# Router logits computed from split token blocks instead of plain tokens, in a fused linear-attention and router kernel

## The chip, the core and the metric

The kernel runs on one core of a Trainium2 chip. A core has five engines that run side by side, each taking its own instructions strictly in order, tied to the others only by semaphores: TensorE (PE in the profile; its weight loads are a row of their own, PEld), VectorE (DVE), ScalarE (ACT), GpSimd (POOL) and SyncE (SP), which here only issues transfers. Matrix products land in eight PSUM banks of 128 x 512 float32. The metric is the device time of one execution in microseconds (us); the profile adds one execution taken apart.

## The reference

Input x is four sequences of 512 tokens with 512 features. After a layer norm, xn goes two ways. One is a decayed linear attention with 16 heads of width 128 (queries, keys, values are silu of projections; a sigmoid gate; an output projection). The other is a router, whose logits the change touches:

```python
logits = jnp.einsum('th,eh->te', flat, router_weight) + router_bias   # 64 experts
scores = jax.nn.softmax(logits, axis=-1)
topk_w, topk_idx = jax.lax.top_k(scores, TOP_K)                       # 8 of 64
out = flat * jnp.sum(topk_w, axis=-1, keepdims=True) + jnp.einsum('tk,tkh->th', topk_w, expert_bias[topk_idx])
```

The result is x + attention * silu(router output).

## The kernel before, in words

**Split products.** Every big product is done in TensorE's float32r form, on numbers split in two: ScalarE casts the high part (`split_hi`, L99, rows of L100), VectorE or GpSimd subtracts it for the low part (`split_lo`, rows of L103). A product takes three passes: high with high, low with high, high with low (`PASSES`, L27).

**Seven products for eight.** The sequences are worked on in two pairs, p = 0 and 1 (`PB` = 2). With the features halved and the two sequences of a pair as the other half, each projection is a 2 x 2 product of blocks: B11 and B12 are the two sequences' first halves of features, B21 and B22 their second halves. It is done in the seven products of `PRODUCTS` (L39) with sums of weights (S1 to S4) and of tokens: T1 = B12 - B11, T2, T3, T4. `unit` (L484) runs the seven, product 0 to product 6, six matmuls each, into three PSUM banks. Product 4 adds onto the bank of product 1, product 5 onto that of product 2, product 6 onto that of 1 and 4. So product 4 waits until VectorE has read its addition "a" from that bank, product 5 until it has read "e", product 6 until it has read the sum of product 4. "a" also needs s1, ScalarE's copy of product 0 (L508).

**Hooks.** A unit takes `after`, seven lists; list i is emitted behind product i. All side work is put there by hand, and that decides its place in each engine's queue. `do_deferred` (L563) emits silu products (VectorE) that wait for ScalarE's sigmoid.

**The v stage** (loop at L947, to about 187 us of the span) has 16 units k = 0 to 15 of 128 tokens from each sequence of a pair. Units 0 to 7 use the first half of the value weights, with p = 0, then p = 1; units 8 to 15 the second half, with p = 1, then p = 0. The first two units are plain products (`plain_unit`, L525; rows of L534) while the weight sums S1 to S4 are being made (`sum_of`, L421; `split_one`, L444; L970 to L975). Units 0 to 6 also prepare the tokens ahead: transposes of tile k + 1 ("turn", rows of L251), ScalarE's copies into xf, sums T1 to T4 on GpSimd (ts, L268), statistics and normalisation of tile k + 2 on VectorE (bn, L226; x, L202; GpSimd makes rstd, L236, in between), splits of the blocks (ACT L100, POOL L103), and the logits. The blocks of p = 1 stay in place at the end of unit 7; from unit 9 those of p = 0 are made again, tile by tile (`combine`), and are complete after unit 12. The value outputs go through four buffers with the tag "vout" to memory.

**Logits before** (`logits`, L310; rows of L318 and L323): for each tile and each sequence, four plain float32 matmuls with the tokens (xf, 128 features x 128 tokens) as the stationary operand and the router weights (128 x 64) as the moving one, so that tokens land on partitions. VectorE adds the bias. Later come the maximum and its subtraction (`scores_less`, L328), the exponentials, and the stores to memory (`scores_exp`, L337), in unit 13. Each exponential on ScalarE needs a table load, and so does going back to sigmoids.

**After the v stage** come units for gate, queries and keys with the attention of the head before (`attention`, L727), each with `scores_qk` (L670), `states` and `attend`; then the output projection (`o_head`, L824; rows of L826), between whose first heads the last head's attention is done (`last_steps`, L1108). `scores_qk` puts scores ("sa") and transposed keys ("kt") into a ring of three banks (`ps_sc`); `attend` has a bank of its own (`ps_o`).

The only lines needed word for word:

```python
lambda: scores_qk(b1, h, attp), lambda: scores_qk(b0, h, attp, (ps_o, "o")),   # L731, heads 0 to 14
[lambda: scores_qk(b1, hl, attp), lambda: scores_qk(b0, hl, attp)],               # L1109, last head
```

Of the kernel before, what the change touches and what calls it, by code (L numbers as in the profile page):

```python
# [18 lines left out]
PB = 2  # L19
# [31 lines left out]
def kernel(  # L51
# [41 lines left out]
    ps_sc = pool(ctx, "ps_sc", 3, space=PSUM)  # L93
    ps_o = pool(ctx, "ps_o", 1, space=PSUM)
# [4 lines left out]
    def split_hi(hi, src):  # L99
        nc.scalar.copy(hi, src)  # L100

    def split_lo(eng, lo, src, hi):
        eng.tensor_tensor(lo, src, hi.bitcast(F32), ALU.subtract)  # L103
# [40 lines left out]

    def warm_up(n):
        ps = ps_o.tile([P, P], F32, tag="o", name="warm")
        for _ in range(n):
            nc.tensor.transpose(ps, ident, ident)  # L150


    def make_dist():
# [36 lines left out]
    blocks = {}  # L190
# [51 lines left out]
    xfs = {}  # L242
# [62 lines left out]
            nc.sync.dma_start(out=blocks_d[n][:, t], in_=blocks[p, n].bitcast(F32)[:, t])  # L305


    lg = {}

    def logits(stage, p, t, js=range(PB)):  # L310
        if t == 0 and 0 in js:
            scores[p] = stage.tile([P, PB, NT, E], F32, tag="scores", name=f"scores_{p}", bufs=2)
        if 0 in js:
            lg[p, t] = ps_sc.tile([P, PB, E], F32, tag="sc", name=f"lg_{p}_{t}")
        ps = lg[p, t]
        for j in js:
            for c in range(FC):
                nc.tensor.matmul(  # L318
                    ps[:, j], xfs[p, t][:, j, c, :], rw[:, c, :], start=(c == 0), stop=(c == FC - 1)
                )  # L320
        if PB - 1 not in js:
            return
        nc.vector.tensor_tensor(  # L323
            scores[p][:, :, t, :], ps, rb[:, None, :].to_broadcast([P, PB, E]), ALU.add
        )


    def scores_less(p, what):  # L328
        sc = scores[p].rearrange("p b t e -> p (b t) e")
        if what == "top":  # L330
            scores[p, "top"] = small.tile([P, PB * NT], F32, tag="top", name=f"top_{p}", bufs=2)
            nc.vector.reduce_max(scores[p, "top"], sc, axis=AX.X)
        else:
            top = scores[p, "top"][:, :, None].to_broadcast([P, PB * NT, E])
            nc.vector.tensor_tensor(sc, sc, top, ALU.subtract)
# [334 lines left out]
    def scores_qk(b, h, attp, psum=(ps_sc, "sc")):  # L670
        s, d = (b, h), dec[b // PB, h]
        q, k = chunks(qs[s]), chunks(ks[s])
        pa = ps_sc.tile([P, NT, P], F32, tag="sc", name=f"sa_{b}_{h}")
        for c in range(NT):
            nc.tensor.matmul(pa[:, c], k[:, c], q[:, c], start=True, stop=True)  # L675
        pk = psum[0].tile([P, NT - 1, P], F32, tag=psum[1], name=f"kt_{b}_{h}")
        for c in range(NT - 1):
            nc.tensor.transpose(pk[:, c], k[:, c], ident)  # L678
        at[s] = attp.tile([P, NT, P], F32, tag="at", name=f"at_{b}_{h}")
        nc.vector.tensor_tensor(  # L680
            at[s], pa, d[:, 0, None, :].to_broadcast([P, NT, P]), ALU.mult
        )
# [154 lines left out]
    def prepare(stage, p, t):  # L837
        first = (p, t) == (0, 0)

        def turn():  # L840
            for j in range(PB):
                transpose(stage, p, j, t)
            if p == 0:
                nc.sync.dma_start(out=xf_d[t], in_=xfs[p, t])

        if p == 0 and t < NP_FIRST:
            sums = (lambda: plain(p, t, nc.vector if t == 0 else nc.gpsimd)), lambda: None, lambda: None
        else:
            sums = combine(stage, p, t, nc.gpsimd)

        def route_logits():
            logits(stage, p, t)
        return {
            "stats": lambda: layer_norms(p, t, first), "norms": lambda: normalise_x(p, t),
            "turn": turn, "sums": sums[0], "plain": sums[1], "more": sums[2], "logits": route_logits,
        }

    def h_units(p, stack):
# [78 lines left out]
    split_blocks(0, 0, nc.vector, (("T1", b12), ("B21", b21), ("B22", b22)))  # L937
    ws[0].split_one("A12", nc.vector, 0)
    ws[0].split_one("A12", nc.gpsimd, 1)
    logits(stage, 0, 0, [0])  # L940
    prep[1]["stats"]()
    prep[1]["norms"]()
    ws[0].split_one("A21", nc.vector)
# [2 lines left out]

    for k, (p, t) in enumerate(tiles + again):  # L947
        g, after = k // n1, nothing()
        for unit_of, what in ((n1 - 3, (0, "top")), (n1 - 2, (0, "less")), (n1 + 2, (1, "top")), (n1 + 3, (1, "less"))):
            if k == unit_of:  # L950
                after[2].append(lambda what=what: scores_less(*what))
        if n1 - NT <= k < n1:
            after[6].append(lambda p=p, t=t: keep_blocks(p, t))
        if k + 1 < n1:
            after[0 if k else 1].append(prep[k + 1]["turn"])
            if 0 < k < n1 - 3:
                after[0].append(lambda k=k: load_pair(stage, *tiles[k + 3]))
            if k == 0:
                after[1].insert(0, prep[2]["stats"])
            after[1].append(prep[k + 1]["sums"])  # L960
            if k + 2 < n1:
                if k:
                    after[1].append(prep[k + 2]["stats"])
                after[4 if k > 1 else 3].append(prep[k + 2]["norms"])
            after[1].append(prep[k + 1]["plain"])
            after[4].append(prep[k + 1]["more"])
            after[4 if k else 6].append(prep[k + 1]["logits"])
        if k == 0:
            after[0].append(lambda: logits(stage, 0, 0, [1]))
        if k < NP_FIRST:  # L970
            for i in range(2 * k, 2 * k + 2):
                after[2 + 2 * (i % 2)].append(lambda i=i: ws[0].sum_of(i, nc.vector))
            for i, n in enumerate((("S1", "S2"), ("S3", "S4"))[k]):
                eng = nc.gpsimd if i else nc.vector
                after[2 * i + 3].append(lambda n=n, eng=eng: ws[0].split_one(n, eng))  # L975
        if k == NP_FIRST:
            after[0].append(ws[1].load())
        if n1 - 5 <= k < n1 - 1:
            after[3].append(lambda n=k - n1 + 5: ws[1].sum_of(n, nc.vector))
        for n, unit_of, step, eng, piece in (  # L980
            ("A11", n1 - 2, 6, nc.gpsimd, None), ("S2", n1 - 1, 0, nc.gpsimd, None),
            ("S1", n1 - 1, 1, nc.gpsimd, None), ("A12", n1 - 1, 2, nc.vector, 0),
            ("S3", n1 - 1, 3, nc.gpsimd, None), ("A12", n1 - 1, 4, nc.vector, 1),
            ("S4", n1, 1, nc.vector, 0), ("S4", n1, 2, nc.vector, 1), ("A22", n1, 0, nc.gpsimd, None),
        ):
            if k == unit_of:
                after[step].append(lambda n=n, eng=eng, piece=piece: ws[1].split_one(n, eng, piece))
        if n1 <= k < n1 + NT:
            after[0].append(lambda t=t: load_xf(stage, t))
        if n1 < k <= n1 + NT:  # L990
            sums, split_plain, split_sums = combine(stage, 0, k - n1 - 1, nc.gpsimd, "r")
            after[1] += [sums, split_plain]
            after[4].append(split_sums)
        if k == NP_FIRST:
            after[0].append(keep_rows)
        if n1 + NT < k < n1 + 2 * NT:
            for j in range(1, len(PRODUCTS)):
                h = (k - n1 - NT - 1) * (len(PRODUCTS) - 1) + j - 1
                if h < NH:
                    after[j].append(lambda h=h: keep_decay(h))  # L1000
        if k == n1 + NT + 1:
            after[1].append(scores_exp)
        if k == 2 * n1 - 2:
            vs_stack.close()
            todo = [(p, *u) for p in range(NP) for u in h_units(p, hw_stack)]
            todo[0][3].load()()
            todo[1][3].load()()
        if k == 2 * n1 - 1:
            weight_steps(todo[0][3], after)
        v_unit(p, g, t, ws[g], vout, after, k < NP_FIRST)  # L1010
# [36 lines left out]
    for i, (p, kind, n, w) in enumerate(todo):  # L1047
# [58 lines left out]
    b1, b0 = B - 1, B - 2  # L1106
    hl = NH - 1
    last_steps = [  # L1108
        [lambda: scores_qk(b1, hl, attp), lambda: scores_qk(b0, hl, attp)],  # L1109
        [lambda: states(b1, hl, attp), lambda: states(b0, hl, attp)],  # L1110
        [lambda: attend(b1, hl, attp), lambda: attend(b0, hl, attp, (ps_sc, "sc"))],
    ]
# [98 lines left out]
```

## Time and profile before

| what | value |
|---|---|
| median of 3 runs | 1064.81 us (1064.03 to 1066.74) |
| profiled execution, its own time | 1063.93 us |
| its span (first to last instruction) | 1062.2 us |
| TensorE clock granted | 0.999 |
| chain that ended last | PE 87%, DVE 1%, all others about 0% |
| old logits, PE rows | 128 records from 9.1 to 97.8 us |
| transfers | 143.11 MB, mean 135 GB/s |

The v units start, by their first weight load, at 9.86 (k = 0), 24.94, 38.49, 51.48, 63.75, 76.00, 88.26, 100.53 (k = 7), 110.05, 120.29, 129.82, 139.34, 148.86, 158.38, 167.90 and 177.42. The next stage begins at 186.94.

How to read it: a row of the profile names the engine, the line of the kernel, the operation, the tile written, the tiles read, the shapes and a count. In a timeline the first two numbers are start and length in us; merged rows have a count, and their length runs from the first start to the last end. What stands in square brackets is the idle time of that engine just before, and what ended it. Rows of one engine may overlap slightly, since the next starts while the last drains: a VectorE row of 0.68 holds its queue for about 0.60. In a table of busy time by stretch the columns are the stretch, its length, and the busy time of PE, PEld, DVE, ACT and POOL, each with its number of instructions.

### The profile page before, as it was taken

To read this page: it belongs to the slowest core of one execution; us is meant where nothing else is said; L and a number is where in the kernel's file an instruction comes from. 1 tells how busy PE (TensorE), PEld (TensorE's weight loads), DVE (VectorE), ACT (ScalarE), POOL (GpSimd) and SP (SyncE) were. 2 spreads that over 40 slices of the span, in tenths; PEclk is the share of its full clock that TensorE was granted. 3 is DMA by queue.
4 is the path that set the end of the run, shared out by engine and by line. 5 is a ranking of instruction groups with operands and counts; after the bars stand their busy time and mean duration, and the time that the engine had idled before them with its cause. 6 is when DMAs were issued, how large, how long until landed. Compare 5 with 4: busy or idle time off the path is not lost.

```text
span 1062.2 us, 16490 instructions
## 1 busy us (share of the span) xinstructions
PE 1053.3 (99%) x5771; PEld 909.4 (86%) x5771; DVE 696.0 (66%) x1061; ACT 476.3 (45%) x923; POOL 728.7 (69%) x710
## 2 busy tenths in 40 slices
PE   9999999999999999999999999999999999999998
PEld 8888788888888888888888888888888888888886
DVE  7898876667576667665756656557566566855464
ACT  5555554544444444444444444444444444332221
POOL 5898893867787678777786787777867857612130
PEclk9999999999999999999999999999999999999999
DMA  6547747522422323235722242232222436455351
GB/s 225 188 176 251 261 148 234 163 85 86 139 85 95 98 92 109 85 124 180 271 85 72 83 125 85 85 123 82 94 72 83 154 128 212 130 170 174 99 186 53
DMA packets 109875, 143.11 MB, mean 135 GB/s; under 512 B 9680, under 2 KB 58208, under 8 KB 108896
## 3 DMA queue, kind: packets, MB, share of 16 engines
q1 hardware_dynamic: 108752, 141.35, 41.0%
q8 instruction: 46, 0.75, 0.3%
q10 hardware_dynamic: 1040, 0.71, 0.2%
q14 instruction: 37, 0.30, 0.1%
HBM read 93.24 MB, written 50.87 MB: 136 GB/s over the span
## 4 chain that ended last, share of the span: by engine, by line
PE 87%; DVE 1%; issue 0%; ACT 0%; POOL 0%; DVEq 0%; ACTq 0%
PE u_qk L502 28%; PE po L826 16%; PE u_g L502 14%; PE u_v L502 7%; PE o L712 5%; PE sa L675 5%; PE ss L698 4%; PE o L714 4%; PE kt L678 2%; PE pu L769 1%; DVE k L558 0%; PE ssq L741 0%; PE pw L388 0%; DVE u L813 0%; POOL sqs L724 0%
## 5 line engine op out<-in xcount | busy, mean ns | idle before, releaser
L826 PE MATMUL po<-wr,yr 128*128 128x512 f32 (+1 forms) x777 | 178.9, 388 | 1.0 <-DVE u L813 1.0
L826 PEld LDWEIGHTS po<-wr,yr 128*128 128x128 f32 x777 | 144.1, 188 | 31.0 <-DVE u L813 1.2
L502 PE MATMUL u_qk<-blk_T,ws_qk 128*128 128x512 f32 x576 | 147.0, 395 | 0.0
L724 POOL TENSOR_TENSOR sqs<-sqs,sq 128x512 f32<-128x512 f32 x60 | 78.9, 1316 | 78.4 <-ACT sq L723 78.4
L502 PEld LDWEIGHTS u_qk<-blk_T,ws_qk 128*128 128x128 f32 x576 | 105.7, 188 | 20.4
L103 POOL TENSOR_TENSOR ws_qk<-sum_qk,ws_qk 128x512 fp32r<-128x512 f32 x64 | 82.8, 1295 | 30.4 <-ACT ws_qk L100 29.5
L502 PE MATMUL u_qk<-blk_B,wa_qk 128*128 128x512 f32 x384 | 99.1, 393 | 0.0
L103 DVE TENSOR_TENSOR yr<-yin,yr 128x512 fp32r<-128x512 f32 x64 | 71.7, 1135 | 39.5 <-ACT yr L100 39.1
L558 DVE TENSOR_TENSOR k<-k,sg_k 128x512 f32<-128x512 f32 x64 | 91.3, 1427 | 2.4 <-ACT sg_k L555 2.2
L712 PE MATMUL o<-at,vin 128*128 128x128 f32 x512 | 88.4, 275 | 0.0
L502 PEld LDWEIGHTS u_qk<-blk_B,wa_qk 128*128 128x128 f32 x384 | 70.9, 188 | 14.2
L702 DVE SCALAR_TENSOR_TENSOR st<-st,bdecay,ss 128x128 f32<-128x128 f32 x128 | 41.7, 347 | 60.4 <-ACT st L700 58.1
L555 ACT ACTIVATE sg_k<-k 128x512 f32<-128x512 f32 x64 | 40.5, 632 | 86.7 <-DVE k L493 86.7
L712 PEld LDWEIGHTS o<-at,vin 128*128 128x128 f32 x512 | 74.9, 191 | 2.5
L502 PE MATMUL u_g<-blk_T,ws_g 128*128 128x512 f32 x288 | 76.0, 399 | 0.0
L714 PE MATMUL o<-qd,st 128*128 128x128 f32 x384 | 74.2, 275 | 0.0
L103 POOL TENSOR_TENSOR ws_g<-sum_g,ws_g 128x512 fp32r<-128x512 f32 x32 | 42.7, 1336 | 44.8 <-ACT ws_g L100 44.8
L777 POOL TENSOR_TENSOR u<-u,sgu 128x512 f32<-128x512 f32 x16 | 20.6, 1290 | 69.7 <-ACT sgu L776 59.8
L716 DVE SCALAR_TENSOR_TENSOR y<-o,nw,gt 128x512 f32<-128x512 f32 x64 | 47.6, 747 | 31.6 <-PE o L714 30.1
L723 ACT ACTIVATE sq<-o 128x512 f32<-128x512 f32 x60 | 35.9, 598 | 71.8 <-POOL sqs L724 43.5
L675 PE MATMUL sa<-q,k 128*128 128x128 f32 x512 | 67.7, 275 | 0.2 <-DVE k L558 0.2
L675 PEld LDWEIGHTS sa<-q,k 128*128 128x128 f32 x512 | 64.3, 191 | 3.5 <-DVE q L558 0.6
(186 smaller groups left out, 2420.8 us busy)
## 6 DMA issues: line engine op xcount, KB each, us to landing
v<-vo_v SPq DMA_DIRECT2D x64, 256.0 KB, 2.1
raw_qk<-in_w_head_dram SPq DMA_DIRECT2D x64, 256.0 KB, 3.5
vin<-v SPq DMA_DIRECT2D x64, 256.0 KB, 3.6
y<-y SPq DMA_DIRECT2D x64, 256.0 KB, 2.0
yin<-y SPq DMA_DIRECT2D x64, 256.0 KB, 3.1
x<-in_x_dram SPq DMA_DIRECT2D x32, 256.0 KB, 4.5
raw_g<-in_w_head_dram SPq DMA_DIRECT2D x32, 256.0 KB, 3.1
raw_v<-in_w_v_dram SPq DMA_DIRECT2D x16, 256.0 KB, 5.7
```

Of the source, the lines that this page charges most:

```text
L103: eng.tensor_tensor(lo, src, hi.bitcast(F32), ALU.subtract)
L502: nc.tensor.matmul(ps, lhsT, rhs, start=(first and c == 0 and n == 0), stop=(c == KC - 1 and n == len(PASSES) - 1), skip_group_check=not f ...
L555: nc.scalar.activation(sg, src, AF.Sigmoid)
L558: nc.vector.tensor_tensor(dst, src, sg, ALU.mult)
L675: nc.tensor.matmul(pa[:, c], k[:, c], q[:, c], start=True, stop=True)
L698: nc.tensor.matmul(ps[:, c], kd[s][:, c], v_of(b, h, c), start=True, stop=True)
L702: nc.vector.scalar_tensor_tensor(r[:, c], r[:, c - 1], bdecay[:, h : h + 1], ps[:, c], ALU.mult, ALU.add)
L712: nc.tensor.matmul(o, v_of(b, h, c), at[s][:, c], start=True, stop=(c == 0))
L714: nc.tensor.matmul(o, st[s][:, c - 1], qd[s][:, c - 1], start=False, stop=True)
L716: nc.vector.scalar_tensor_tensor(y, po, nw[:, h : h + 1], gts[s], ALU.mult, ALU.mult)
L724: nc.gpsimd.tensor_tensor(sq[b], sq[b], s1, ALU.add)
L826: nc.tensor.matmul(pos[t][:, c], yr[:, yi, bass.ts(t, P)], wos[h][:, wi, c], start=(h == 0 and n == 0), stop=(h in stops and n == len(PASS ...
```

## The change

1. **Logits from blocks.** The router weights are split into a high and a low part once, side by side (128 columns: 64 high, 64 low), as the stationary operand. The moving operand is a split block for all four tiles of a pair, 512 tokens wide, its high part, then its low part. So high and low products of the 64 experts land on 128 partitions, tokens along the free side. Sequence 0 of the pair is B11 and B21; sequence 1 is T1 and B22 plus what B11 gave (since B12 = T1 + B11). That is 16 matmuls for a pair. ScalarE and VectorE move the two sums to SBUF, in the "vout" buffers; eight transposes turn them back; VectorE adds bias, then high and low.
2. **Places.** The old logits leave units 0 to 6. The new ones stand in unit 8 for p = 1 and in unit 13 for p = 0: products and rest behind products 0 and 1, turns behind 2 and 3, maximum behind 4, subtraction behind 5. The exponentials and their stores move from behind product 1 to behind product 6 of unit 13. The weight split stands behind product 2 of unit 7.
3. **Stand-ins.** The two halves of the first tile's logits become eight transposes each of the same tile (`warm_up` with `src`), whose result is not used.
4. **The fourth weight sum** S4, made in unit 1, moves from behind its third group of products to its end, behind the last silu of the unit, and its split follows.
5. **Last head's keys**: the second sequence's transposed keys go to the bank of `ps_o`.

```diff
-    def warm_up(n):
+    def warm_up(n, src=ident):
...
-            nc.tensor.transpose(ps, ident, ident)
+            nc.tensor.transpose(ps, src, ident)
...
+    def split_rw(stage):
+        rwr.append(stage.tile([P, FC, 2, E], F32R, tag="rwr", name="rwr", bufs=1))
+        split_hi(rwr[0][:, :, 0], rw)
+        split_lo(nc.vector, rwr[0][:, :, 1], rw, rwr[0][:, :, 0])
...
+    def logits(stage, p, outp):
+        ps, sb = {}, {}
+
+        def part(j, k, n, first=False, last=False, more=False):
+            if first:
+                ps[j] = ps_sc.tile([P, N], F32, tag="sc", name=f"lg_{p}_{j}")
+            for c in range(KC):
+                for xi in range(2):
+                    nc.tensor.matmul(
+                        ps[j], rwr[0][:, k * KC + c].rearrange("p a e -> p (a e)"), blocks[p, n][:, :, xi, c],
+                        start=(first and c == 0 and xi == 0), stop=(last and c == KC - 1 and xi == 1),
+                        skip_group_check=more,
+                    )
...
+        def products():
+            part(0, 0, "B11", True, True)
+            nc.scalar.copy(temp("s1"), ps[0])
+            part(1, 0, "T1", True)
+            part(1, 1, "B22", False, True)
+            nc.vector.tensor_tensor(temp("l1"), ps[1], sb["s1"], ALU.add)
+
+        def rest():
+            part(0, 1, "B21", False, True, True)
+            nc.scalar.copy(temp("l0"), ps[0])
+
+        def turn(j):
...
+            pl = ps_sc.tile([P, NT, 2, E], F32, tag="sc", name=f"lt_{p}_{j}")
+            for t in range(NT):
+                nc.tensor.transpose(
+                    pl[:, t].rearrange("p a e -> p (a e)"), sb[f"l{j}"][:, bass.ts(t, P)], ident
                 )
...
+            nc.vector.tensor_tensor(sc, pl[:, :, 1], rb[:, None, :].to_broadcast([P, NT, E]), ALU.add)
+            nc.vector.tensor_tensor(sc, pl[:, :, 0], sc, ALU.add)
+        return [products, rest, lambda: turn(1), lambda: turn(0)]
...
-    logits(stage, 0, 0, [0])
+    warm_up(8, xfs[0, 0][:, 0, 0])
...
-            after[4 if k else 6].append(prep[k + 1]["logits"])
         if k == 0:
-            after[0].append(lambda: logits(stage, 0, 0, [1]))
+            after[0].append(lambda: warm_up(8, xfs[0, 0][:, 1, 0]))
+        if k == n1 - 1:
+            after[2].append(lambda: split_rw(stage))
+        for unit_of, p2 in ((n1, 1), (n1 + NT + 1, 0)):
+            if k == unit_of:
+                less = [lambda p2=p2, what=what: scores_less(p2, what) for what in ("top", "less")]
+                for j, f in enumerate(logits(stage, p2, vout) + less):
+                    after[j].append(f)
         if k < NP_FIRST:
-            for i in range(2 * k, 2 * k + 2):
-                after[2 + 2 * (i % 2)].append(lambda i=i: ws[0].sum_of(i, nc.vector))
...
+                steps = (6, 6) if (k, i) == (1, 1) else (2 * i + 2, 2 * i + 3)
+                if steps[0] == 6:
+                    after[6].append(do_deferred)
...
         if k == n1 + NT + 1:
-            after[1].append(scores_exp)
+            after[6].append(scores_exp)
...
-        [lambda: scores_qk(b1, hl, attp), lambda: scores_qk(b0, hl, attp)],
+        [lambda: scores_qk(b1, hl, attp), lambda: scores_qk(b0, hl, attp, (ps_o, "o"))],
```

More of the change, by code (lines that the diff above doesn't have):

```diff
@@ L305, in keep_blocks @@
             nc.sync.dma_start(out=blocks_d[n][:, t], in_=blocks[p, n].bitcast(F32)[:, t])
[L308 to L319, printed above, removed]
-                )
[L321 to L325, printed above, removed]
+    rwr = []
@@ new lines, in split_rw, with temp @@
+    def split_rw(stage):
[14 more added lines that the diff above has]
+                    )
+        def temp(n):
+            sb[n] = outp.tile([P, N], F32, tag="vout", name=f"lg_{n}_{p}")
+            return sb[n]
+        def products():
[8 more added lines that the diff above has]
+        def turn(j):
+            if j == PB - 1:
+                scores[p] = stage.tile([P, PB, NT, E], F32, tag="scores", name=f"scores_{p}", bufs=2)
+            pl = ps_sc.tile([P, NT, 2, E], F32, tag="sc", name=f"lt_{p}_{j}")
+            for t in range(NT):
+                nc.tensor.transpose(
+                    pl[:, t].rearrange("p a e -> p (a e)"), sb[f"l{j}"][:, bass.ts(t, P)], ident
+                )
+            sc = scores[p][:, j]
+            nc.vector.tensor_tensor(sc, pl[:, :, 1], rb[:, None, :].to_broadcast([P, NT, E]), ALU.add)
+            nc.vector.tensor_tensor(sc, pl[:, :, 0], sc, ALU.add)
+        return [products, rest, lambda: turn(1), lambda: turn(0)]
@@ L849, in prepare @@
             sums = combine(stage, p, t, nc.gpsimd)
-        def route_logits():
-            logits(stage, p, t)
         return {
             "stats": lambda: layer_norms(p, t, first), "norms": lambda: normalise_x(p, t),
-            "turn": turn, "sums": sums[0], "plain": sums[1], "more": sums[2], "logits": route_logits,
+            "turn": turn, "sums": sums[0], "plain": sums[1], "more": sums[2],
         }
@@ L948 @@
         g, after = k // n1, nothing()
-        for unit_of, what in ((n1 - 3, (0, "top")), (n1 - 2, (0, "less")), (n1 + 2, (1, "top")), (n1 + 3, (1, "less"))):
-            if k == unit_of:
-                after[2].append(lambda what=what: scores_less(*what))
         if n1 - NT <= k < n1:
@@ L966 @@
             after[4].append(prep[k + 1]["more"])
-            after[4 if k else 6].append(prep[k + 1]["logits"])
         if k == 0:
-            after[0].append(lambda: logits(stage, 0, 0, [1]))
-        if k < NP_FIRST:
-            for i in range(2 * k, 2 * k + 2):
-                after[2 + 2 * (i % 2)].append(lambda i=i: ws[0].sum_of(i, nc.vector))
-            for i, n in enumerate((("S1", "S2"), ("S3", "S4"))[k]):
-                eng = nc.gpsimd if i else nc.vector
-                after[2 * i + 3].append(lambda n=n, eng=eng: ws[0].split_one(n, eng))
+            after[0].append(lambda: warm_up(8, xfs[0, 0][:, 1, 0]))
[6 more added lines that the diff above has]
+                    after[j].append(f)
+        if k < NP_FIRST:
+            for i in range(2):
+                n, eng = f"S{2 * k + i + 1}", nc.gpsimd if i else nc.vector
+                steps = (6, 6) if (k, i) == (1, 1) else (2 * i + 2, 2 * i + 3)
+                if steps[0] == 6:
+                    after[6].append(do_deferred)
+                after[steps[0]].append(lambda i=2 * k + i: ws[0].sum_of(i, nc.vector))
+                after[steps[1]].append(lambda n=n, eng=eng: ws[0].split_one(n, eng))
         if k == NP_FIRST:
```

## The prediction

> **What bounds the kernel now.** I read the page's first part, then busy time unit by unit in the v stage, then who waits inside one unit. The page says that TensorE never rests:
>
> ```profile
> PE 1053.3 (99%) x5771; PEld 909.4 (86%) x5771; DVE 696.0 (66%) x1061; ACT 476.3 (45%) x923; POOL 728.7 (69%) x710
> ```
>
> So a TensorE microsecond removed looks like a microsecond gained. But those are means over stages. The busy time by unit (columns: PE, PEld, DVE, ACT, POOL) shows units 3, 4 and 5, which still prepare tokens, and then unit 10, which doesn't:
>
> ```profile
> 51.48:63.75 12.27, 12.27 (x68) 10.50 (x66) 11.97 (x21) 6.08 (x14) 12.11 (x14) 1.00 0.75 264
> 63.75:76.00 12.25, 12.25 (x68) 10.50 (x67) 11.77 (x20) 6.07 (x14) 11.06 (x14) 1.00 0.36 130
> 76.00:88.26 12.26, 12.26 (x68) 10.50 (x67) 11.44 (x20) 6.08 (x14) 10.72 (x14) 1.00 0.66 236
> 129.82:139.34 9.52, 9.52 (x44) 7.88 (x43) 7.17 (x11) 5.00 (x14) 9.22 (x12) 1.00 0.46 167
> ```
>
> In units 3 to 5 VectorE and GpSimd are within 0.3 to 1.5 us of TensorE: the stage has three engines near their limit, and the old logits sit there. The timelines of unit 4 and of the seam between units 1 and 2 say how far TensorE is ahead (start, length, engine):
>
> ```profile
> 71.45 1.98 PEld L318 LDWEIGHTS lg<-rw,xf 128*128 128x128 f32 x16
> 72.21 0.68 DVE L493 TENSOR_TENSOR vo_v<-u_v,e_v 128x512 f32<-128x512 f32 x1
> 74.61 1.35 PEld L502 LDWEIGHTS u_v<-w_A_v,blk_T 128*128 128x128 f32 x6
> ...
> 40.71 1.54 DVE L438 TENSOR_TENSOR sum_v<-raw_v,sum_v 128x1024 f32<-128x1024 f32 x1
> 42.29 1.05 ACT L100 CAST w_S_v<-sum_v 128x1024 fp32r<-128x1024 f32 x1 [2.79 <-DVE sum_v L438]
> 42.91 1.23 PEld L502 LDWEIGHTS u_v<-w_S_v,blk_T 128*128 128x128 f32 x6 [0.85 <-DVE vo_v L558]
> 43.51 2.55 POOL L103 TENSOR_TENSOR w_S_v<-sum_v,w_S_v 128x512 fp32r<-128x512 f32 x2
> ...
> 160.99 1.28 ACT L339 ACT_TABLE_LOAD   x1
> 162.28 1.15 ACT L339 ACTIVATE scores<-scores 128x512 f32<-128x512 f32 x2
> ...
> 871.14 0.31 PEld L678 LDWEIGHTS kt<-ident,k 128*128 128x128 f32 x3 [1.51 <-DVE at L680]
> ```
>
> Product 6 (74.61) accumulates in the bank that VectorE reads for product 4's sum, ready at 72.21 + 0.68 = 72.89. TensorE has 1.72 us to spare there, and the logits supply it.
>
> **TensorE's bill.** Old logits: a block of 8 matmuls (16 records) holds the queue 73.34 - 71.45 = 1.89 us; seven full blocks, 13.3 us. The first tile's two halves (0.9 and 1.0 us) become 8 transposes each; the warm-up's six at 8.32 took 0.65 to the next instruction, so 0.87: nothing gained, they wait for the same weights. New logits, twice: 16 matmuls of 512 columns at 9.52/42 = 0.227 make 3.63, 8 transposes as in a turn (66.11 - 65.11) make 1.0: 4.6, together 9.2. TensorE alone gains 4.1. The question is whether units 1 to 7 can give back 13.3, since units 8 and 13 certainly take 9.2.
>
> **Units 1 to 7: the cover goes.** VectorE loses only seven score additions (0.28, 0.20 of its queue each) and, in units 5 and 6, a maximum (0.6) and a subtraction (0.7). Unit 1's own end comes 3 us sooner (two blocks less, then a wait for GpSimd's tile-1 remainders, busy 22.88 to 26.5). From 29.34 to 67.13 GpSimd has no idle row, whatever TensorE does, so unit 2 can't follow.
>
> The moved fourth sum makes it worse. Two silus now go first: they free product 2's bank (the 0.85 wait goes), but the sum starts about 0.8 later, at 41.5, and so does its cast on ScalarE, and behind that cast in ScalarE's queue stand unit 2's s1 copy and the copies of tile 3. VectorE's addition "a" of unit 2 (43.86) waits for s1: 44.65. GpSimd's split of S4, 43.51 to 46.06, becomes 44.2 to 46.75; behind it stand tile 3's sums, the rstd that VectorE's normalisation needs (49.63 becomes 50.4) and B11 of unit 3. What was 0.85 of TensorE wait returns as 0.7 on the two engines with no slack. The rows from there, shifted: VectorE is 0.55 late in unit 2, 0.35 in unit 3 and 0.15 at unit 4's "a" (0.2 less per score addition, 0.18 where it waited for TensorE). Unit 4's product-4 sum then ends at 73.05, product 6 follows and ends at 74.4 instead of 76.0. Unit 5: less 0.2, less 0.52 (an idle gap), less 0.6: sum 84.98, end 86.35 instead of 88.26. Unit 6 is light on VectorE (9.89 of 12.27): TensorE's own 12.27 - 1.89 = 10.4, end 96.75 instead of 100.53. Unit 7 waits for T2, the last tile's second block: its sums follow the xf copies, behind unit 5's last silus on VectorE (now 1.36 earlier: 91.6 for 92.97); 4.3 + 2.1 + 1.0 of GpSimd work later T2 is there at 99.0. Unit 7: 98.75 + 6 x 1.36 = 106.9 instead of 110.05. So **3.1 us come back**, not 13.3.
>
> A rule speaks to this. The Trainium skill (SBUF — State Buffer, "SBUF: two separate sides") says that VectorE and GpSimd hold a shared port pair by turns, and the loser waits out the other's whole instruction. The rows agree: two normalisations take 1.00 us at 16.19 with GpSimd idle, 2.00 at 73.41. If one hoped that the lock eases, units 3 to 5 could shed about 1.0 on these and 0.45 on a silu (1.13 against 0.68), and come near TensorE's 10.4; by the rule the lock stays as long as GpSimd has 11 us per unit. I keep the rows.
>
> **Unit 8.** It now lasts 10.24 with 0.72 of waits for weights split late by GpSimd and VectorE (rows at 115.64 to 119.03). The new logits lie between its products, so those waits vanish: 9.52 + 4.6. End: 106.9 + 14.1 = 121.0, against 120.29: **+0.7**. The extra VectorE work (one addition, four of 256 columns, maximum, subtraction: some 3.5 us) and ScalarE's three copies lie beside that longer unit; without that cover product 5 would wait for S4. The weight split before it (128x256, about 0.4 on each of two engines) is in a unit with VectorE 7.46 of 9.52: nothing.
>
> **Unit 13: +4.6.** TensorE has no wait in units 9 to 15, so all is paid. The blocks it reads are complete: GpSimd's last split ends at 162.1, T1 of it at 160.0, about when the second product's pass asks.
>
> **Exponentials.** They move to the end of unit 13. ScalarE has then the last sigmoid, a table load (1.28), two exponentials (1.15), and unit 14's s1 copy behind them; maximum and subtraction hold back the last two sums on VectorE by 0.6 and 0.7. Before, that sigmoid starts 1.2 after the unit's end; now about 2.0, so s1 is ready at about 5.6 and "a" at 6.4, where product 4 could start at 4 x 1.36 = 5.44: **+1.0**. The Trainium skill (ScalarE: Activation LUTs, "What ACT_TABLE_LOAD costs") adds 1.38 of drain per switch, which would make it 2.4; here the exponential starts at 162.28, 1.29 after the load's start, so no drain shows: by the row 1.0. No lower than 0, if ScalarE catches up. On SP the four score stores now stand behind the decay copies and before raw_g, raw_qk and unit 13's last v store. raw_g lands some 2.6 us later against the units; its sums had from 177.43 to 184.46 before the first S weights: hidden. The late v store frees its buffer about 1 us before unit 14's last sum wants it.
>
> **Tail: -1.4.** The keys' transposes wait 1.51 for a bank that VectorE reads; the outputs' bank is last read by the square at 865.58, so 1.5 goes; at 890.11 TensorE waits 0.26 for a weight of GpSimd's, of which some 0.1 may come back. After that the products follow with no other limit.
>
> **Sum.** 0.7 + 4.6 + 1.0 - 1.4 = +4.9 on the profiled execution (1063.93, span 1062.2): 1068.8. The median of the runs, 1064.81, is 0.88 above it: **1069.7**.
>
> **Rivals.** *TensorE alone bounds (chance 0.13, faster).* If VectorE needs no more than 10.4 a unit in units 3 to 5, all cover is real: -13.3 + 9.2 - 0.85 - 0.72 - 1.4 = -7.1, 1057.7. For: the chain of waits names almost only PE. Against: VectorE's 11.4 to 12.0. It decides from about 1.1 us less VectorE and GpSimd time per unit. *Part of it (0.25).* The freed order costs the lock 0.4 a unit less in units 2 to 7 (2.4) and the S4 delay of 0.7 is absorbed: +4.9 - 3.1 = +1.8, 1066.6; inside noise. *A stall in unit 8 (0.10).* The new temporaries share the ring of the v tiles; if ScalarE's copy waits for a store (VectorE waits up to 1.6 for one now) with S4's cast behind it, and the drain shows: 1.6 + 1.4 more, 1072.7. The forecast has 0.52.
>
> **Chances and range.** About 0.3%, 3.2 us, is what a measurement here can tell from no change. Faster is the first rival, 0.13; within is the second with a little of the forecast's edge, 0.27; slower 0.60. The range runs from 1062.5 (part of it, with nothing lost at the exponentials and more shed) to 1073.0.
>
> **What would show it.** PE busy below 95% in units 2 to 7, with waits for "vo_v", "e_v" and blocks; unit 8 starting near 107 and ending near 121; unit 13 at 14.1 long; a gap before unit 14's product 4; none at "kt". I am wrong if units 3 to 5 shrink to 10.4, or if GpSimd's S4 split doesn't move.

## The result, and the profile after

| | median, us | runs from, to |
|---|---|---|
| before (7 runs) | 1064.33 | 1063.68 to 1066.74; one at 2168.11 |
| changed (7 runs) | 1069.63 | 1068.99 to 1073.23 |

The ratio is 1.0054, with an interval from 1.0038 to 1.0070: the change costs about 5 us. The execution taken apart took 1072.0 us (span 1070.2). It starts late (the last section says why), as some executions of both kernels do. Its unit 1 comes 1.9 to 2.2 us, in the mean 2.05, behind that of seven traces of the experiments below, which have the same first unit and start on time. So its times from unit 1 on are read less 2.05. That makes its own time about 1069.95, just above the five runs without such a start (1068.99 to 1069.86).

The page of the changed kernel, first part and chain of waits:

```profile
PE 1053.7 (98%) x5707; PEld 904.7 (85%) x5707; DVE 697.9 (65%) x1064; ACT 478.6 (45%) x928; POOL 729.9 (68%) x710
...
PE 88%; POOL 5%; DVE 3%; DMA 1%; issue 1%; ACT 1%; SPq 0%; POOLq 0%; DVEq 0%; ACTq 0%
```

TensorE is as busy as before in a longer span, and the chain, which before named almost only PE (87%, DVE 1%), now passes through GpSimd and VectorE. Busy time by unit (start:end, length, then PE, PEld, DVE, ACT, POOL), units 3, 4, 5 and 11:

```profile
52.59:64.28 11.69, 11.08 (x52) 8.55 (x51) 11.31 (x19) 5.52 (x13) 11.53 (x14) 1.00 0.85 293
64.28:75.65 11.37, 10.97 (x51) 8.62 (x50) 10.99 (x19) 6.07 (x15) 11.21 (x14) 1.00 0.41 139
75.65:87.02 11.37, 11.04 (x52) 8.64 (x51) 10.98 (x19) 6.08 (x15) 11.21 (x14) 1.00 0.70 254
141.73:151.25 9.52, 9.52 (x44) 7.88 (x42) 6.58 (x10) 5.01 (x14) 9.20 (x12) 1.00 0.48 165
```

Each of units 3 to 5 lost a logits block of 1.89 us but is only 0.6 to 0.9 shorter; VectorE and GpSimd fill what is left. PE itself looks busy because its rows are stretched: the matmuls of unit 4 are 10.97 us busy here, and the same matmuls 10.40 in the version of experiment 6 where TensorE hardly waits. That is why its 98% says so little. In units 3 to 5 TensorE waits 0.46 to 0.74 us for a token block of GpSimd's (T2) and 0.60 to 0.65 for the sum of VectorE's that product 6 needs; in unit 4 (start, length, engine; what an instruction waited for in brackets):

```profile
67.31 2.34 PEld L533 LDWEIGHTS u_v<-w_S_v,blk_T 128*128 128x128 f32 x11 [0.49 <-POOL blk_T L103]
...
74.39 1.23 PEld L533 LDWEIGHTS u_v<-w_A_v,blk_T 128*128 128x128 f32 x6 [0.65 <-DVE vo_v L524]
```

Which of the two engines holds the unit is for experiment 6 to say. The seam between units 1 and 2:

```profile
43.73 1.26 DVE L469 TENSOR_TENSOR sum_v<-raw_v,sum_v 128x1024 f32<-128x1024 f32 x1
45.02 1.04 ACT L100 CAST w_S_v<-sum_v 128x1024 fp32r<-128x1024 f32 x1 [4.52 <-DVE sum_v L469]
45.97 0.58 ACT L539 COPY s_v<-u_v 128x512 f32<-128x512 f32 x1
46.14 2.54 POOL L103 TENSOR_TENSOR w_S_v<-sum_v,w_S_v 128x512 fp32r<-128x512 f32 x2 [0.57 <-ACT w_S_v L100]
...
46.60 1.23 PEld L533 LDWEIGHTS u_v<-w_A_v,blk_B 128*128 128x128 f32 x6 [2.11 <-ACT s_v L539]
```

The moved sum holds its cast, the cast holds s1, and product 3 of unit 2 waits 2.11 us for s1. The end of unit 13 and the two units behind it:

```profile
177.58 1.28 ACT L370 ACT_TABLE_LOAD   x1
...
178.87 1.15 ACT L370 ACTIVATE scores<-scores 128x512 f32<-128x512 f32 x2
179.53 1.77 SPq L372 DMA_DIRECT2D scd<-scores  x4
179.93 0.56 ACT L539 COPY s_v<-u_v 128x512 f32<-128x512 f32 x1
...
180.54 1.23 PEld L533 LDWEIGHTS u_v<-w_A_v,blk_B 128*128 128x128 f32 x6 [1.65 <-ACT s_v L539]
...
183.88 0.81 SPq L449 DMA_DIRECT2D raw_qk<-in_w_head_dram  x2
184.73 0.43 SPq L619 DMA_DIRECT2D v<-vo_v  x1
...
189.29 0.69 DVE L524 TENSOR_TENSOR vo_v<-u_v,a_v 128x512 f32<-128x512 f32 x1 [3.05 <-DMA v<-vo_v]
...
191.23 1.23 PEld L533 LDWEIGHTS u_v<-w_A_v,blk_B 128*128 128x128 f32 x6 [1.29 <-ACT s_v L539]
```

There are two stalls. Unit 14's product 3, which adds onto the bank that s1 is copied from, waits for s1, and s1 stands behind the exponentials. Unit 15's waits for s1 as well, but that began at VectorE: its last sum of unit 14 (189.29) waits 3.05 us until the store issued at 184.73 has landed and its buffer is free; the sigmoid of that sum stands ahead of s1 on ScalarE. In the tail TensorE's waits (in total, times, longest) no longer name the keys' bank:

```profile
PEld sa L706 <- PE kt L709: 0.4, 1, 0.4
PEld po L857 <- POOL wr L103: 0.3, 1, 0.3
```

The length of the units, and where the difference stands (changed, less 2.05 from unit 3 on; difference is changed less before):

| point | before | changed | difference |
|---|---|---|---|
| unit 3 starts | 51.48 | 50.54 | -0.9 |
| unit 8 starts | 110.05 | 106.52 | -3.5 |
| unit 9 starts (unit 8: 10.24, then 14.08 long) | 120.29 | 120.60 | +0.3 |
| unit 14 starts (unit 13: 9.52, then 14.08) | 167.90 | 172.80 | +4.9 |
| unit 15 starts (unit 14: 9.52, then 11.04) | 177.42 | 183.84 | +6.4 |
| next stage (unit 15: 9.52, then 10.69) | 186.94 | 194.53 | +7.6 |
| end of the span | 1062.2 | 1068.15 | +6.0 |

### The profile page after: what moved, and what is told of

Same layout as the page of the kernel before. It is cut to its first block, busy times and chain, and to the rows that moved or that the text cites. A ratio compares the mean times of both kernels' runs of the same rounds, so it can differ in the third digit from the quotient of the medians.

```text
span 1070.2 us, 16366 instructions
## 1 busy us (share of the span) xinstructions
PE 1053.7 (98%) x5707; PEld 904.7 (85%) x5707; DVE 697.9 (65%) x1064; ACT 478.6 (45%) x928; POOL 729.9 (68%) x710
## 4 chain that ended last, share of the span: by engine, by line
PE 88%; POOL 5%; DVE 3%; DMA 1%; issue 1%; ACT 1%; SPq 0%; POOLq 0%; DVEq 0%; ACTq 0%
PE u_qk L533 28%; PE po L857 16%; PE u_g L533 14%; PE u_v L533 6%; PE o L743 5%; PE sa L706 5%; PE o L745 4%; PE ss L729 4%; PE kt L709 2%; POOL ts L268 2%; POOL blk_T L103 2%; POOL blk_B L103 1%; DMA raw_v<-in_w_v_dram 1%; PE pu L800 1%; PE lg L324 1%
## 5 line engine op out<-in xcount | busy, mean ns | idle before, releaser
L533 PEld LDWEIGHTS u_qk<-blk_B,wa_qk 128*128 128x128 f32 x384 | 70.9, 188 | 14.1
```

The costliest lines, as they stand in the source:

```text
L533: nc.tensor.matmul(ps, lhsT, rhs, start=(first and c == 0 and n == 0), stop=(c == KC - 1 and n == len(PASSES) - 1), skip_group_check=not f ...
```

## The experiments

Theory A is that of the prediction: TensorE, VectorE and GpSimd all bound units 2 to 7, so little of 13.3 us comes back, and what the new logits and the moved steps cost in later units is paid. Rival B is that TensorE alone bounds, so that something else must have eaten the gain. Ratios are to the kernel before, on the same chip.

**1. The tail edit alone**, on the kernel before:

```diff
-        [lambda: scores_qk(b1, hl, attp), lambda: scores_qk(b0, hl, attp)],
+        [lambda: scores_qk(b1, hl, attp), lambda: scores_qk(b0, hl, attp, (ps_o, "o"))],
```

> The kernel before with the tail edit alone: the last head's second pair of scores and keys goes to the outputs' bank. My theory: the 1.51 us wait of the keys' transposes goes and nothing follows it but 0.1 us, so 1.4 us less than before: 1062.9 us against 1064.3. The rival: another wait takes its place at once (the weights of GpSimd at the last heads), so no difference, 1064.3 us.

Measured: 1062.71 us (12 runs), ratio 0.9982 [0.9973, 0.9990]. Its span is 1060.7 against 1062.2, so 1.5 us of wait went and nothing came in its place. This kernel is faster than both.

**2. The S4 move alone**, on the kernel before:

```diff
-                after[2 + 2 * (i % 2)].append(lambda i=i: ws[0].sum_of(i, nc.vector))
...
+                steps = (6, 6) if (k, i) == (1, 1) else (2 * i + 2, 2 * i + 3)
+                if steps[0] == 6:
+                    after[6].append(do_deferred)
```

> The kernel before with the fourth weight sum and its split moved behind the two silus, and nothing else. The old logits are still there as cover in units 2 to 7. My theory: TensorE's 0.85 us wait for product 2's bank goes, GpSimd's S4 split starts about 0.7 us later, and since units 3 to 5 are bounded here by TensorE with 0.3 to 1.5 us of slack on the other two, the time is between 0.85 less and 0.4 more: about 1064.0 us. The rival, that the move costs its delay whatever the cover: 0.7 us more, 1065.0 us. In the trace GpSimd's S4 split at about 44.2 instead of 43.51 by both.

Measured: 1066.41 us (21 runs), ratio 1.0017 [1.0011, 1.0024]: 1.2 to 2.6 us slower, more than either account allowed. (Seven of its runs lie a good 2 us above the others, as some of before do; without these on either side the difference is about 1.5.) Its timeline says why:

```profile
45.79 1.24 PEld L502 LDWEIGHTS u_v<-w_A_v,blk_B 128*128 128x128 f32 x6 [1.83 <-ACT s_v L508]
```

Product 2's wait of 0.85 goes, but product 3 waits 1.83 for s1: +1.0, and unit 2 is 14.02 long instead of 12.99. I had looked only at "a", which product 4 needs; product 3 adds onto the bank that the s1 copy reads. Unit 8 is also 0.84 longer there, with 1.00 of wait for "a"; what sets that off was not traced.

**3. The S4 move undone** in the changed kernel:

> The changed kernel with the fourth weight sum and its split put back to their old places. My theory, that what the move saves on TensorE it costs on VectorE and GpSimd, which bound the units behind: 0.7 us less than the changed kernel's 1069.6, so 1068.9 us. The rival, that the bank wait was real and the move pays: 0.85 us more, 1070.5 us. If the delay is absorbed and the wait as well, no difference.

Measured: 1069.65 us (5 runs), ratio 1.0041 [1.0029, 1.0054], not separable in time from the changed kernel. The timeline has the exchange in plain sight: the bank wait is back, and the one for s1 is gone.

```profile
42.96 1.23 PEld L533 LDWEIGHTS u_v<-w_S_v,blk_T 128*128 128x128 f32 x6 [1.83 <-DVE vo_v L589]
```

Unit 3 starts at 49.91 against 50.35 in an on-time trace with the move (run 7), unit 9 at 120.14 against 120.42. But unit 2, which begins before the move has any effect, starts 0.25 us later in this trace (35.19 against 34.94). So the move costs 0.7 us by unit 3 and 0.5 by unit 9, close to theory A's 0.7.

**4. The old logits left out** in the kernel before, VectorE's additions reading a constant (the first tile's two halves become transposes, as in the change):

```diff
-            for c in range(FC):
-                nc.tensor.matmul(
-                    ps[:, j], xfs[p, t][:, j, c, :], rw[:, c, :], start=(c == 0), stop=(c == FC - 1)
-                )
...
-            scores[p][:, :, t, :], ps, rb[:, None, :].to_broadcast([P, PB, E]), ALU.add
+            scores[p][:, :, t, :], *[rb[:, None, :].to_broadcast([P, PB, E])] * 2, ALU.add
```

> The kernel before with the old logits' matmuls left out (their additions read a constant instead, so VectorE and GpSimd have the same work; the first tile's two halves are replaced by transposes as in the changed kernel); the router's result is therefore not computed. It measures what units 1 to 7 can give back of 13.3 us of TensorE time when VectorE and GpSimd keep all their work. My theory, that these two bound units 2 to 7 at once: 3 to 4 us less than before, 1060.3 to 1061.3 us, with unit 8 starting near 106.5 and TensorE waiting for VectorE's sums and GpSimd's blocks. The rival, that TensorE alone bounds: 13.3 us less, 1051 us, unit 8 near 97.

Measured: 1065.91 us (13 runs), ratio 1.0001 [0.9992, 1.0010]: no gain in the median. Eight of the 13 runs lie at 1065.75 or above, among them the profiled one, which starts late; the other five lie at 1063.13 to 1064.27, about 0.8 us below the on-time runs of before. That is far from rival B's 13.3, but the run is no clean measure of A: the stand-in addition reads two operands in on-chip memory and takes 0.82 us, where the one from PSUM takes 0.28. Before, then here:

```profile
75.33 0.28 DVE L323 TENSOR_TENSOR scores<-lg,rb 128x128 f32<-128x128 f32 x1
```

```profile
66.97 0.82 DVE L317 TENSOR_TENSOR scores<-rb 128x128 f32<-128x128 f32 x1
```

So it loads VectorE with 0.5 us more in each unit. (The Trainium skill, SBUF — State Buffer, "Who interferes with whom", says that a VectorE instruction contends with GpSimd's reads if both of its inputs are in SBUF and not if only one is; these two rows agree.)

**5. A quarter of the old logits**, which leaves VectorE and GpSimd exactly as they were:

```diff
-            for c in range(FC):
+            for c in range(1):
                 nc.tensor.matmul(
-                    ps[:, j], xfs[p, t][:, j, c, :], rw[:, c, :], start=(c == 0), stop=(c == FC - 1)
+                    ps[:, j], xfs[p, t][:, j, c, :], rw[:, c, :], start=True, stop=True
```

> The kernel before with one of the four matmuls of every old logits product (three quarters of the router's sum left out); every other instruction stays, so VectorE and GpSimd have exactly their old work, and TensorE has 6 x 0.236 = 1.4 us less in each of seven units, 9.9 us in all. It mends the earlier run without any logits, whose stand-in additions read on-chip memory and took 0.82 us instead of 0.28 under GpSimd's subtractions. My theory, that VectorE (11.2 of 11.4 us busy in units 3 to 5 of the changed kernel, GpSimd close behind) bounds at once: about 2 us less than before, 1062.4 us, unit 8 starting near 108 instead of 110.05. The rival, that TensorE alone bounds: 9.9 us less, 1054.5 us, unit 8 near 100.

Measured: 1063.07 us (21 runs), ratio 0.9982 [0.9974, 0.9990]. Of 9.9 us taken from TensorE 1.1 to 2.8 come back, so rival B is out. Units 4 and 5:

```profile
63.10:74.97 11.87, 11.38 (x55) 9.15 (x54) 11.57 (x20) 6.06 (x15) 10.68 (x13) 1.00 0.39 133
74.97:87.22 12.25, 11.44 (x56) 9.16 (x55) 11.95 (x22) 6.09 (x15) 11.05 (x14) 1.00 0.66 237
```

Unit 5 lasts 12.25 us, as with all of its logits (12.26): VectorE, which has the maximum to do there, is busy for 11.95.

**6. Which engine is it?** Three versions of the changed kernel take work from GpSimd (the low part of T4, zeroed once at the start), from VectorE (the normalisation of the second pair) and from both:

```diff
-            split_lo(eng, blk[:, 1], src, blk[:, 0])
+            if n != "T4":
+                split_lo(eng, blk[:, 1], src, blk[:, 0])
...
-        for b in range(p * PB, p * PB + PB):
+        for b in range(p * PB, p * PB + PB) if p == 0 else ():
             normalise(xts[b, t], xts[b, t], b, t)
```

> The changed kernel without the low part of the token block T4 (zero instead; GpSimd's subtraction for it is left out in every tile, so that part of the product is missing): GpSimd has 1.07 us less in each unit from 2 on, 10.3 instead of 11.37 in units 3 to 5, just under TensorE's 10.4. VectorE's work is unchanged. My theory, that GpSimd's queue bounds units 2 to 7 (it has no idle row between 46 and 118 us): these five or six units shed up to 1 us each until TensorE or VectorE bounds, 3 to 5 us in all, 1065 to 1066.5 us. The rival, that VectorE bounds there and GpSimd only keeps step with it: less than 1 us, 1068.6 to 1069.6 us.

> The changed kernel without the normalisation of the second pair's tokens (they go raw into its products, so that half of the result is not the reference's): VectorE has 1.83 us less in each of units 2 to 5, and nothing else changes. My theory now, that VectorE bounds units 3 to 5 with 11.2 of 11.37 us busy: these fall to about 10.4 to 10.6, where TensorE (7 x 1.36 + 0.9) or GpSimd takes over, 2.5 to 3.5 us in all by unit 8: 1066.3 to 1067.2 us. The rival, that GpSimd (contiguous from 46 to 118 us) is an equal bound: less than 1 us, 1068.6 to 1069.6 us.

> The changed kernel with both of the earlier reliefs: no low part of T4 (GpSimd 1.07 us less in each unit) and no normalisation of the second pair's tokens (VectorE 1.83 us less in units 2 to 5); that part of the result is not the reference's. Alone, the first made units 4 and 5 11.26 us long and the second 11.0, against 11.37. My theory, that VectorE and GpSimd bound together through their shared access to on-chip memory: with both relieved GpSimd needs about 9.9 and VectorE 9.5, so units 4 and 5 fall to TensorE's own 10.4, more than the two gains added (0.97 against 0.11 + 0.39), and the time to 1066.5 to 1067.3 us. The rival, that some third thing (ScalarE's casts, the order of the silus) holds these units: 10.9 or longer, no more than the second alone, 1068.1 us.

Measured: GpSimd relieved 1069.36 us, ratio 1.0046 [1.0033, 1.0058]; VectorE relieved 1068.14, 1.0028 [1.0017, 1.0040]; both 1068.32 (on time 1067.5 to 1068.6), 1.0036 [1.0022, 1.0049]. Unit 4 in each, in this order:

```profile
62.16:73.43 11.27, 10.94 (x52) 8.56 (x51) 10.97 (x19) 6.08 (x15) 10.07 (x13) 1.00 0.41 140
```

```profile
62.30:73.30 11.00, 10.71 (x52) 8.63 (x50) 9.60 (x17) 5.98 (x15) 10.84 (x14) 1.00 0.41 144
```

```profile
61.80:72.20 10.40, 10.40 (x52) 8.58 (x51) 8.97 (x17) 5.93 (x15) 9.96 (x12) 1.00 0.44 152
```

With GpSimd at 10.07 the unit still takes 11.27, with VectorE at 10.97. With VectorE at 9.60 it takes 11.00, with GpSimd at 10.84. Only with both down does it reach TensorE's own 10.4. With GpSimd relieved, TensorE's waits for GpSimd's block are gone from the unit and those for VectorE grow from 0.65 to 1.1 us. So VectorE binds this unit first, GpSimd stands 0.4 us behind it, and TensorE another 0.6 behind that. The two are coupled: GpSimd's same work takes 10.84 us instead of 11.21 once VectorE's normalisations are gone. My guess for the first run, that GpSimd's unbroken row of work makes it the bound, was wrong: a row without gaps doesn't show that the engine is the limit. The forecasts for the other two runs were too low in time. I had 10.4 to 10.6 a unit for the second, and had not seen that units 3 and 7 keep their length: even with both relieved they last 11.75 and 10.80 us (11.69 and 10.70 in the changed kernel), with 1.23 us of wait for GpSimd's block in the one and 1.41 for VectorE's sum in the other.

**7. The store first.** In the changed kernel, unit 13's last silu and its store go ahead of the exponentials:

```diff
-            after[6].append(scores_exp)
+            after[6] += [do_deferred, scores_exp]
```

> The changed kernel with one thing moved: unit 13's last silu and with it the store of its value tile are emitted ahead of the exponentials and the four score stores instead of behind them and behind the loads of raw_g and raw_qk on SyncE's queue. The trace of the changed kernel has unit 15 1.17 us longer than before, where VectorE waits 3.05 us for the landing of that store. My theory now: the store leaves at about 178.3 instead of 184.73, the buffer is free in time, and 1.2 us go: 1068.4 us. The rival, that the late sigmoids and table loads on ScalarE make unit 15 late: no difference, 1069.6 us.

Measured: 1068.75 us (5 runs), ratio 1.0050 [1.0037, 1.0062]; its on-time runs lie at 1068.50 to 1068.75, those of the changed kernel at 1068.99 to 1069.86. SyncE's queue and TensorE's only wait behind unit 12:

```profile
176.16 0.53 SPq L619 DMA_DIRECT2D v<-vo_v  x1
177.29 1.88 SPq L372 DMA_DIRECT2D scd<-scores  x4
```

```profile
PEld u_v L533 <- ACT s_v L539: 1.6, 1, 1.6
```

The store leaves ahead of the scores, unit 15 is 9.52 long again, and the changed kernel's second wait (2.9 us in two) is gone. Unit 14 keeps its own. The medians alone would not settle 1 us; the trace does. The size differs between executions: in six other traces with the store behind, unit 15's wait lies between 0.28 and 1.44 us.

**8. The price of the new matmuls.** In the changed kernel 12 of 16 are left out, in unit 8 (shown) and, with p == 0, in unit 13:

```diff
-            for c in range(KC):
-                for xi in range(2):
+            some = (1, 1) if p == 1 else (KC, 2)
+            for c in range(some[0]):
+                for xi in range(some[1]):
...
```

> The changed kernel with 12 of the 16 matmuls of the new logits left out in unit 8 (the first pair to be done, so its router logits are not computed in full): prices them. My theory, that unit 8 is bounded by TensorE and pays for every matmul: 12 x 0.227 = 2.7 us less, 1066.9 us, less up to 0.7 us of waits for the weights split late, which come back: 1066.9 to 1067.6 us. The rival, that VectorE or GpSimd bound unit 8 too: less than 1 us, 1068.6 to 1069.6 us.

> The changed kernel with 12 of the 16 matmuls of the new logits left out in unit 13 (the other pair's router logits are then not computed in full). My theory: TensorE has no wait in units 9 to 13, so all of it comes back, 12 x 0.227 = 2.7 us: 1066.9 us. The rival, that the exponentials, the score stores or the blocks' splits then wait in its place: 1 us or more is lost again, 1067.9 us and above.

Measured: unit 13's 1067.10 us (7 runs), ratio 1.0030 [1.0016, 1.0043], unit 13 is 11.39 long instead of 14.08: all 2.7 us. Unit 8's 1069.04 us, ratio 1.0046 [1.0033, 1.0058], and unit 8 is 13.39 long: only 0.7 of 2.7. There I was wrong. TensorE's rows in that unit 8:

```profile
110.39 0.19 PEld L325 LDWEIGHTS lg<-blk_B,rwr 128*128 128x128 f32 x1 [0.33 <-ACT lg_s L337]
...
112.11 0.42 PEld L351 LDWEIGHTS lt<-ident,lg_l 128*128 128x128 f32 x4 [0.25 <-DVE lg_l L340]
...
117.43 0.19 PEld L534 LDWEIGHTS u_v<-w_S_v,blk_B 128*128 128x128 f32 x1 [0.74 <-DVE w_S_v L103]
118.82 1.23 PEld L534 LDWEIGHTS u_v<-w_A_v,blk_T 128*128 128x128 f32 x6 [1.21 <-DVE vo_v L525]
```

With few matmuls, VectorE's split of S4 and its sums come late at once. Unit 8 is 3.15 us longer than before even with only four matmuls of logits. Of the 2.5 us of waits in these rows 2.2 are for VectorE and 0.3 for ScalarE, so VectorE sets the price of this unit nearly as much as TensorE does.

## Why the prediction was right, and where it wasn't

The forecast, 1069.7, is the measured time. The mechanism of most steps held, but part of the closeness is luck. The forecast stood on a median of three runs, 1064.81; seven give 1064.33, so the change costs 5.3 us by the medians, where +4.9 was forecast, and a baseline 0.5 too high made up for it. And two terms were too small, others too large: from profile to profile they add up to +6.0 (execution less its late start).

- **Units 1 to 7 give back 3.1, not 13.3.** Right: 3.5 by the start of unit 8. Run 5 shows it without the rest of the change, run 6 names the engines. The predicted order was VectorE first, through the sum that product 6 waits for; run 6 confirms it for units 4 and 5. For unit 7 the forecast was that GpSimd's T2 holds it until 99.0; it came at 98.66. Between them errors cancelled: unit 5 is 11.37 long where I had 11.95, but units 6 and 7 are 10.85 and 10.70 where I had 10.4 and 10.15. One sign I had named did not show: PE busy below 95% (it is 95 to 97% in units 3 to 5, since its rows stretch while it waits).
- **S4: 0.85 saved, 0.7 lost elsewhere.** The delay of GpSimd's split is there (2.6 us later in the trace, 0.6 of it beyond the late start), but the step that lets VectorE's addition "a" of unit 2 wait for s1 missed a second victim: TensorE's product 3 waits for it too, 1.83 us in run 2 and 2.11 in the changed kernel. Against the kernel with the move undone the loss is 0.5 to 0.7 us (run 3), so the size was right.
- **Unit 8: 14.1 long, end +0.7.** Measured 14.08 and +0.3, since unit 8 also began 0.4 sooner than forecast. That 4.6 is TensorE's price was right only as long as the matmuls are there; run 8 shows that VectorE's share is close behind. The rows of before told it: VectorE has no gap in that unit (10.24 of 10.24 us), and two of the waits that I put down to late weights (0.18 and 0.40) name its sums.
- **Unit 13: +4.6.** Measured +4.56, and run 8 shows that it is TensorE's: the 12 matmuls left out bring back their whole 2.7.
- **Exponentials: +1.0.** Measured +1.52. The times of the sigmoid (2.08 after the unit's start) and of s1 (5.64, predicted 5.6) were right, but I let product 4 wait (from 5.44) where product 3 waits (from 4.08): 5.64 - 4.08 = 1.56. The same mistake as at S4: the bank that a product accumulates into was read off for products 4 to 6, not for 3. The choice of the row over the 1.38 us of drain that the Trainium skill states (ScalarE: Activation LUTs, "What ACT_TABLE_LOAD costs") held: the exponential starts 1.29 us after its table load (177.58 to 178.87), so no drain shows. No run moves the exponentials; this account is read from the rows.
- **Unit 15: nothing.** Failed: +1.17. The step was "the late v store frees its buffer about 1 us before unit 14's last sum wants it". I had counted the issue times on SyncE's queue, not its waits: the score stores wait 1.1 us for the exponentials, and raw_qk's load waits 1.5 us until they have landed, all ahead of the v store, which is issued at 184.73 where the silu was done by 178.28. Run 7 shows it; the size, 1.17, is this execution's.
- **Tail: -1.4.** Measured -1.6 (+7.6 at the next stage, +6.0 at the end), and -1.5 in span by itself (run 1).
- **The rivals.** TensorE alone is excluded by run 5. "Part of it" needed the lock to ease by 0.4 a unit; in unit 4 it came to about 0.25 by the rows (the two normalisations 1.83 us instead of 2.00, one silu 0.68 instead of 1.13, but a weight sum 1.59 instead of 1.22), and units 14 and 15 lost more than that. No copy waited for a store in unit 8.

## What to carry to other kernels

Work taken from a full engine is worth only the distance to the next engine in that same stage; where three engines stand within a microsecond, move the same work to a stage where one engine has slack, or leave it. When a step is moved, list for each product which bank it adds onto and who reads that bank, and follow the in-order queue of every engine past each wait in it, not only past each issue. Try the parts of a mixed change one by one: here one line of it (the tail's bank) is worth 1.5 us, and the rest costs nearly 7.

## What was not expected of the hardware

**The start is late in some executions, and the traces point to a race for on-chip memory.** Both kernels have executions about 2 us longer than the rest: in experiment 2's set, 7 of the 40 runs of before lie at 1066.03 or above, the others at 1065.13 or below. In the profiled execution of the changed kernel and in the on-time one of run 7, VectorE and GpSimd in unit 0 (start, length):

```profile
16.43 2.68 POOL L103 TENSOR_TENSOR w_A_v<-raw_v,w_A_v 128x512 fp32r<-128x512 f32 x2
16.50 2.89 DVE L202 TENSOR_SCALAR x<-x,stats,rstd 128x512 f32<-128x512 f32 x2 [0.82 <-POOL rstd L236]
```

```profile
16.16 1.00 DVE L202 TENSOR_SCALAR x<-x,stats,rstd 128x512 f32<-128x512 f32 x2 [0.82 <-POOL rstd L236]
...
17.59 3.18 POOL L103 TENSOR_TENSOR w_A_v<-raw_v,w_A_v 128x512 fp32r<-128x512 f32 x2 [1.47 <-ACT w_A_v L100]
```

In the first the weights of A22 were cast before the normalisation was ready to go; GpSimd's subtraction starts 0.07 us ahead of it, and the normalisation takes 2.89 us instead of 1.00, for which TensorE's turn of tile 1 waits. So weights that come sooner can make the whole later. No late execution of the kernel before was profiled, but experiment 4's late trace, of a kernel made from it, has the like at the next step: GpSimd's subtraction starts at 17.00, VectorE's own for A21 at 17.14, and that takes 3.47 us; in the profile of before VectorE's starts first (17.11 against 17.27) and takes 1.29. The Trainium skill (SBUF — State Buffer, "Who interferes with whom") says that the order of issue decides who is blocked, and these rows agree. One more run, the quarter-logits kernel with that subtraction on VectorE:

```diff
-    ws[0].split_one("A22", nc.gpsimd)
+    ws[0].split_one("A22", nc.vector)
```

> The same with a quarter of the old logits, and in the first unit the low part of the weights A22 is subtracted by VectorE instead of GpSimd. In the traces so far the start is 2 to 2.3 us later in some executions: there VectorE's normalisation of tile 1 takes 2.89 us for the pair instead of 1.00, or its A21 subtraction 3.47 instead of 1.28, whenever GpSimd's A22 subtraction (two of 128x512) begins shortly before it. My theory: with GpSimd idle there this can't happen, and no execution lies 2 us above the others; the median is within 1.5 us of the quarter-logits kernel's fast start, since VectorE has 1.3 us more to do in unit 0. The rival, that the late start comes from the arrival of the first transfers: late executions remain, 2 us above the others, in about one of four.

Measured: 1064.22 us, ratio 0.9990 [0.9981, 0.9998], and its 13 runs lie between 1063.11 and 1064.90, where the 21 of the quarter-logits kernel lie between 1061.79 and 1066.87. No run is long any more, at a price of 1.2 us in the median. That supports the race, but doesn't settle it: only two of the 21 were more than 2 us above their median, and 13 without one could be chance.
